# The last attention's schedule: projections in odd steps, prologue pieces in even ones, an earlier normalisation, the output bias as a weight row and the mask in parts

## The chip, the cores and the metric

The kernel runs on one core of a Trainium2 chip. Its time is the device time of the whole program on that core, in microseconds (us). The core has five engines that work beside each other: TensorE (PE, with its weight loads shown as PEld), VectorE (DVE), ScalarE (ACT), GpSimd (POOL) and SyncE (SP), which issues the transfers. Each engine takes its instructions in order, and an instruction waits for what others must have written or freed. Everything here is float32.

## The reference

The input is x, 8 batches of 512 rows with 256 columns. Four layers follow one another, each with its own normalisation and added to x: an attention (a), a feed-forward block with local attention, a second attention (b), and the feed-forward block again. Only attention b is changed. It has 16 heads of 16 columns, a score that is no plain product, and a bias on its output:

```python
    def _L0_attn_b_ref(x, w_qkv, b_qkv, w_out, b_out):
        ...
        qkv = x @ w_qkv + b_qkv
        q, k, v = jnp.split(qkv, 3, axis=-1)
        ...
        dot = jnp.einsum('bhid,bhjd->bhij', q, k)
        q_norm_sq = jnp.sum(q * q, axis=-1, keepdims=True)
        k_norm_sq = jnp.sum(k * k, axis=-1, keepdims=True)
        vals = q_norm_sq + k_norm_sq.transpose(0, 1, 3, 2)
        scores = dot * dot / (vals - 2.0 * dot + EPSILON) * SCORE_SCALE
        mask = jnp.triu(jnp.ones((Lq, Lq), dtype=scores.dtype), k=1) * -1000000000.0
        scores = scores + mask[None, None, :, :]
        attn = jax.nn.softmax(scores, axis=-1)
        out = jnp.einsum('bhij,bhjd->bhid', attn, v)
        out = out.transpose(0, 2, 1, 3).reshape(Bq, Lq, E)
        return out @ w_out + b_out
    ...
    x = x + _L0_attn_b_ref(_layernorm(x, axis=-1), L0_attn_b_w_qkv, L0_attn_b_b_qkv, L0_attn_b_w_out, L0_attn_b_b_out)
```

## The kernel before

The eight batches are done in two groups of four, whose rows stay in SBUF (`xs`). A group passes through ten stages: attention a, two layers of local attention and feed-forward, attention b (`attention_b`, L946), and two such layers again. Each stage gives a head and a function `run`; in its last steps `run` calls `ahead`, which writes the next stage's head in between.

**Units and steps.** In attention b a batch is cut into 22 units. A unit is a block of 128 query rows (`i`, 0 to 3) with a pair of heads from each of several groups of four heads (`js`): for `i` = 0 there are two units of four pairs, for `i` = 1 four units of two pairs, for `i` = 2 and 3 eight units of one pair each. With the causal mask a block `i` needs `i` + 1 blocks of keys, so each unit has 1024 scores in a row (768 for `i` = 2). `each_part` (L1253) writes one step, in which up to six units are in work at different depths: the denominators of unit s (`product`, then `inverse` on ScalarE, `error` and `refine` on VectorE), the square of the dot product of unit s-1 (`squares`, L1112, which also adds the mask `causal` on POOL at L1116), the maximum of unit s-2 (`highest`, L1119, VectorE) and its exponentials on ScalarE, the transposes of unit s-3 in two halves, each copied to SBUF by VectorE (`keep_turned`, L1157), and in odd steps the products with the values of units s-5 and s-4 (`values`).

**Pieces.** Each step may take one piece of other work, cut into up to four parts that are put in between: `first` on TensorE, `act` on ScalarE, `second` on TensorE, `dve` on VectorE. There are two kinds:

- *Projections* (`project`, L1184). When all heads of a block `i` are done, the reciprocal of the sums is spread on POOL, and two pieces follow: one turns the reciprocals and divides (`oT`, L1205), one multiplies by the output weights (`pp`, L1210) and adds to x (L1215). They come up in steps 5, 9, 17 of a batch and in step 3 of the next.
- *The prologue of the next batch* (`stacks_and_values`, L964): one piece that turns the normalised rows into columns, eight *side pieces* (`side_piece`, L981) that make the stacks for q and k, marked heavy, with TensorE, ScalarE, TensorE and VectorE in a chain (`pu_b` L987, `sq_b` L997, `pu_b` L1000, `st_b` L1013), and two *value pieces* (`value_piece`, L1024).

Ahead of the prologue come two pieces that only VectorE and POOL work on (`normalized`, L949): the statistics (four `bn_stats` and aggregates, then two POOL instructions for the inverse root), and the rows (`yr`), with the output bias then added to x on POOL (L959).

**Which piece a step takes** is decided by `a_piece` (L1246):

```python
if projections:
    return projections.popleft()
if prologues and not norms and not (with_values and prologues[0].heavy):
    return prologues.popleft()
```

So a projection always goes first, and a heavy piece never goes into a step with value products, which is every odd step from the fifth on. At the start of a batch (`step % each == 0`, L1308) what is left of its prologue is written out at once, piece after piece (`whole`, L1059); I call this the drain. Only then do `norms` and `prologues` get the pieces of the batch after it. `kept_order` makes the order in which the steps are written the order on every engine.

**Buffers.** Denominators, dot products and the pieces share three PSUM buffers (`ps_s`); the transposes have one (`ps_mm`).

Of the kernel before, what the change touches and what calls it, by code (L numbers as in the profile page):

```python
# [17 lines left out]
P = 128  # L18
NB, T, D = 8, 512, 256
NT = T // P  # L20
GROUP = 4
H, HD = 8, 64
HB, HDB = 16, 16
# [21 lines left out]
def kernel(  # L45
# [12 lines left out]
    b_wv,  # L58
    b_bv,
    b_wo,  # L60
    b_bo,
    f_wqkv,
    f_scale,
    f_wo,
# [38 lines left out]
    def part(flat, at, shape):  # L103

        n = int(np.prod(shape))
        view = flat[:, at : at + n]
        if len(shape) == 2:
            view = view.rearrange("p (k n) -> p k n", n=shape[1])
        return view, at + n

    def fetch(src, dst, rows=True):
        nc.sync.dma_start(dst, src.rearrange("(k p) n -> p k n", p=P) if rows else src.partition_broadcast(P))
# [55 lines left out]
    def weights_b(name):  # L168
        flat = wts.tile([P, 4096], F32, tag="wa", name=f"wb_{name}", bufs=2)
        wl, at = part(flat, 0, (2, INNER))  # L170
        wr, at = part(flat, at, (2, INNER))
        wv, at = part(flat, at, (2, D))
        wo, at = part(flat, at, (4, D))
        bv, at = part(flat, at, (D,))
        bo, at = part(flat, at, (D,))
        for s, d in ((b_wl, wl), (b_wr, wr), (b_wv, wv), (b_wo, wo)):
            fetch(s, d)
        fetch(b_bv, bv, False)
        fetch(b_bo, bo, False)
        return wl, wr, wv, wo, bv, bo  # L180


    ident = const.tile([P, P], F32, name="ident")
# [760 lines left out]


    def attention_b(batches, g):  # L946
        wl_b, wr_b, wv_b, wo_b, bv_b, bo_b = weights_b(g)

        def normalized(b):  # L949

            got = {}

            def statistics():
                got["mv"], got["rstd"] = row_statistics([xs[b]], f"b{b}")

            def rows():
                yr = pool.tile([P, NT, D], F32, tag="yr", name=f"yr_b{b}", bufs=1)
                normalize_rows([xs[b]], [yr], got["mv"], got["rstd"])
                nc.gpsimd.tensor_add(xs[b], xs[b], bo_b.unsqueeze(1).to_broadcast([P, NT, D]))  # L959
                state[b] = {"yr": yr}  # L960

            return [Piece(False, dve=statistics), Piece(False, dve=rows)]

        def stacks_and_values(b):  # L964


            got = {}

            def turned():
                got["pt"] = ps_s.tile([P, 2, NT, P], F32, tag="s", name=f"pyt_b{b}")  # L970
                for k in range(2):
                    for t in range(NT):
                        nc.tensor.transpose(got["pt"][:, k, t, :], state[b]["yr"][:, t, k * P : (k + 1) * P], ident)

            def columns():
                got["yT"] = pool.tile([P, 2, T], F32, tag="hT", name=f"yT_b{b}")
                nc.scalar.copy(got["yT"], got.pop("pt").rearrange("p k t c -> p k (t c)"))

            yield Piece(False, first=turned, act=columns)

            def side_piece(side, w, j):  # L981
                vec = vec_b[:, side, j, :]

                def project():
                    got["pu"] = ps_s.tile([P, 2, T], F32, tag="s", name=f"pu_b{b}_{side}_{j}")[:, 0]
                    for k in range(2):
                        nc.tensor.matmul(  # L987
                            got["pu"],
                            lhsT=w[:, k, j * P : (j + 1) * P],
                            rhs=got["yT"][:, k, :],  # L990
                            start=(k == 0),
                            stop=(k == 1),
                        )

                def squared():
                    got["sq"] = pool.tile([P, T], F32, tag="two", name=f"sq_b{b}_{side}_{j}", bufs=5)
                    nc.scalar.activation(got["sq"], got["pu"], AF.Square, bias=vec[:, 0:1])  # L997

                def norms():
                    nc.tensor.matmul(  # L1000
                        got["pu"],
                        lhsT=sel_b[:, side, :],
                        rhs=got.pop("sq"),
                        start=False,
                        stop=True,
                        skip_group_check=True,
                    )

                def keep_side():
                    name = ("left", "right")[side]  # L1010
                    if name not in state[b]:
                        state[b][name] = big([P, 4, T], f"st_b{b}_{side}")
                    nc.vector.tensor_scalar(  # L1013
                        state[b][name][:, j, :], got.pop("pu"), vec[:, 0:1], vec[:, 1:2], ALU.add, ALU.mult
                    )

                return Piece(True, project, squared, norms, keep_side)

            for side, w in ((0, wl_b), (1, wr_b)):
                for j in range(4):  # L1020
                    yield side_piece(side, w, j)


            def value_piece(t2):  # L1024
                def project():
                    got["pv"] = ps_s.tile([P, 2, 2, HB * HDB], F32, tag="s", name=f"pv_b{b}_{t2}")
                    for i in range(2):
                        t = 2 * t2 + i
                        for k in range(2):
                            nc.tensor.matmul(  # L1030
                                got["pv"][:, i, 0],
                                lhsT=got["yT"][:, k, t * P : (t + 1) * P],
                                rhs=wv_b[:, k, :],
                                start=(k == 0),
                                stop=(k == 1),
                            )

                def keep_values():
                    if t2 == 0:
                        state[b]["v"] = pool.tile([P, NT, (HB + 1) * HDB], F32, tag="v", name=f"v_b{b}")  # L1040
                        nc.gpsimd.memset(state[b]["v"][:, :, HB * HDB :], 0.0)
                    pv = got.pop("pv")
                    for i in range(2):
                        nc.vector.tensor_add(state[b]["v"][:, 2 * t2 + i, : HB * HDB], pv[:, i, 0], bv_b)

                return Piece(False, first=project, dve=keep_values)

            for t2 in range(NT // 2):
                yield value_piece(t2)
# [16 lines left out]
        def unit(b, i, qp, js, first, last):  # L1066
# [8 lines left out]
            def per_head(t):  # L1075
                return t[:, :, :cols].rearrange("p a (m w) -> p a m w", w=width)
# [35 lines left out]
            def squares(dot):  # L1112
                num = pool.tile([P, 2, T], F32, tag="p", name=f"num_{n}", bufs=3)
                nc.scalar.activation(num[:, :, :cols], dot[:, :, :cols], AF.Square, scale=-0.5)  # L1114
                own = per_head(num)[:, :, :, past:]
                nc.gpsimd.tensor_add(own, own, causal.unsqueeze(1).unsqueeze(1).to_broadcast([P, 2, len(js), P]))  # L1116
                return num

            def highest(num, r):  # L1119
# [109 lines left out]
        def run(ahead):  # L1229
# [13 lines left out]
                        if k < len(some):  # L1243
                            some[k]()

            def a_piece(with_values):  # L1246
                if projections:
                    return projections.popleft()
                if prologues and not norms and not (with_values and prologues[0].heavy):
                    return prologues.popleft()  # L1250
                return Piece(False)

            def each_part(s):  # L1253
# [6 lines left out]
                if with_values:  # L1260
                    for u in (s - 5, s - 4):
                        projections.extend(units[u].project(sums.pop(u)))
                piece = a_piece(with_values)

                def do(part):
                    if part:
# [40 lines left out]
            for step in range(count + 5):  # L1307
                if step % each == 0:  # L1308
                    with kept_order():
                        while prologues or norms:  # L1310
                            whole((norms or prologues).popleft())
                    following = step // each + 1
                    if following < len(batches):
                        norms.extend(normalized(batches[following]))
                        prologues = deque(stacks_and_values(batches[following]))
                with kept_order():
                    each_part(step)
                if step > count - 6:
                    ahead()
# [48 lines left out]
def laid_out(inputs):  # L1368
# [17 lines left out]
    vec = vec.reshape(2, 4, P, 2).transpose(2, 0, 1, 3)  # L1386
    wo_b = np.zeros((HB, 2, HDB, D), f)
    wo_b[:, 0] = i["L0_attn_b_w_out"].reshape(HB, HDB, D)

    qs, ks = i["L0_ffn_q_scale"], i["L0_ffn_k_scale"]  # L1390
    swapped = lambda s: np.concatenate([s[:, HD // 2 :], s[:, : HD // 2]], 1)
# [2 lines left out]
    for half, rest in ((0, 0), (1, GATES)):  # L1394
# [17 lines left out]
        "b_wv": wqkv[:, 2 * D :],  # L1412
        "b_bv": bias[2 * D :],
        "b_wo": wo_b.reshape(INNER, D),
        "b_bo": i["L0_attn_b_b_out"],
        "f_wqkv": i["L0_ffn_wqkv"],
        "f_scale": np.stack([qs, swapped(qs), ks, swapped(ks)], 1),
        "f_wo": i["L0_ffn_wo"],
# [25 lines left out]
```

## Time and profile before

| | |
|---|---|
| median of 3 runs | 4722.27 us (4718.59 to 4723.31) |
| profiled execution | 4716.77 us, span 4715.0 us |
| granted TensorE clock, mean | 0.963 |
| busy: PE, PEld | 4385.6 us (93%), 2660.9 us (56%) |
| busy: DVE, ACT, POOL | 3177.9 us (67%), 2243.9 us (48%), 1275.0 us (27%) |
| attention b, first group | from about 1081 to 1600 us |
| attention b, second group | from about 3425 to 3950 us |

The page divides the span into 40 slices of 118 us; each digit is the tenths of a slice in which the engine was busy. Attention b lies in slices 9 to 13 and 29 to 33, counted from 0. The rows of its instruction groups name the line, the engine, the tile written and the tiles read; their mean is in nanoseconds. The answers of the trace that are used below are of three kinds: busy times of each engine in chosen stretches, with the granted clock (PEclk, 1.00 is full speed); VectorE's waits, as "who waited <- for what: us in total, times, longest"; and instructions in order of time, with start, duration and, in brackets, the idle time in front and what ended it.

### The profile page before, as it was taken

How to read it: one execution, taken by the hardware profiler on the slowest of the kernel's cores; microseconds unless marked ns; L12 is line 12 of the kernel's file. 1: busy time of each engine (PE TensorE's matmuls, PEld its weight loads, DVE VectorE, ACT ScalarE, POOL GpSimd, SP SyncE). 2: the span in 40 equal slices, each digit the busy share in tenths (PEclk: the TensorE clock that was granted, in tenths of full speed). 3: DMA queues.
4: the chain of work that ended last, by engine and by line, in shares of the span. 5: the costliest groups of instructions: out<-in, count | busy, mean ns of one | idle time of the engine just before them, and what ended most of it. 6: DMA issues, size and time to landing. Idle time of an engine off the chain costs nothing. (4 is left out here: it accounts for less than half of the span.)

```text
span 4715.0 us, 68722 instructions
## 1 busy us (share of the span) xinstructions
PE 4385.6 (93%) x26240; PEld 2660.9 (56%) x26240; DVE 3177.9 (67%) x7400; ACT 2243.9 (48%) x5228; POOL 1275.0 (27%) x1164
## 2 busy tenths in 40 slices
PE   9999999997777899999999999999977778999999
PEld 5666656654444466566566666566544444665665
DVE  5667637738998777377456686476389887863772
ACT  3345425417877654155133453254178775541541
POOL 0014314312222243133100242243122222431431
PEclk9999999999988799999999999999989887999999
DMA  2000000000000000000100000000000000000000
GB/s 77 1 21 3 23 21 3 21 5 19 1 1 1 19 3 5 4 21 12 49 28 1 19 3 23 21 3 23 2 19 1 1 1 19 3 6 21 3 4 23
DMA packets 50922, 63.17 MB, mean 13 GB/s; under 512 B 6257, under 2 KB 45345, under 8 KB 50593
## 3 DMA queue, kind: packets, MB, share of 16 engines
q1 hardware_dynamic: 50592, 58.77, 3.8%
q8 instruction: 208, 3.41, 0.3%
q14 instruction: 122, 0.99, 0.1%
HBM read 46.19 MB, written 4.19 MB: 11 GB/s over the span
## 5 line engine op out<-in xcount | busy, mean ns | idle before, releaser
L1154 PE MATMUL ppt_b<-ident,num_b 128*128 128x128 f32 x1280 | 249.4, 318 | 200.4 <-DVE pt_b L1159 157.7
L1154 PEld LDWEIGHTS ppt_b<-ident,num_b 128*128 128x128 f32 x1280 | 155.4, 157 | 383.6 <-ACT num_b L228 133.0
L1116 POOL TENSOR_TENSOR num_b<-num_b,causal 128x256 f32<-128x256 f32 (+2 forms) x176 | 172.0, 977 | 695.3 <-ACT num_b L1114 525.1
L228 ACT ACTIVATE p_a<-s_a,nm_a 128x512 f32<-128x512 f32 x256 | 173.8, 683 | 304.1 <-DVE nm_a L384 304.1
L228 ACT ACTIVATE num_b<-num_b,most_b 128x512 f32<-128x512 f32 (+3 forms) x512 | 280.7, 553 | 50.4 <-DVE most_b L1134 47.4
L1124 DVE CUSTOM_DVE_ANT_0 num_b<-num_b,r_b 128x512 f32<-128x512 f32 (+3 forms) x512 | 263.9, 562 | 4.6 <-POOL num_b L1116 4.6
L1085 PE MATMUL den_b<-st_b,st_b 18*128 18x384 f32 (+3 forms) x1024 | 238.6, 523 | 7.3 <-DVE t_b L1104 5.1
L1159 DVE COPY pt_b<-ppt_b 128x512 f32<-128x512 f32 (+1 forms) x352 | 223.3, 634 | 29.6 <-PE ppt_b L1154 28.5
L228 ACT ACTIVATE r_b<-den_b 128x1024 f32<-128x1024 f32 (+1 forms) x176 | 166.5, 946 | 150.1 <-PE den_b L1085 96.9
L1085 PE MATMUL dot_b<-st_b,st_b 16*128 16x384 f32 (+3 forms) x1024 | 216.0, 525 | 1.9 <-ACT num_b L1114 1.4
L228 ACT ACTIVATE p_f1y<-p_f1y,nm_f1y,rn_f1y 128x256 f32<-128x256 f32 (+1 forms) x256 | 143.7, 563 | 137.5 <-DVE nm_f1y L617 125.7
L228 ACT ACTIVATE p_f0y<-p_f0y,nm_f0y,rn_f0y 128x256 f32<-128x256 f32 (+1 forms) x256 | 143.7, 564 | 137.3 <-DVE nm_f0y L617 125.7
L228 ACT ACTIVATE p_f0x<-p_f0x,nm_f0x,rn_f0x 128x256 f32<-128x256 f32 (+1 forms) x256 | 143.7, 564 | 130.1 <-DVE nm_f0x L617 118.4
L228 ACT ACTIVATE p_f1x<-p_f1x,nm_f1x,rn_f1x 128x256 f32<-128x256 f32 (+1 forms) x256 | 143.7, 564 | 129.9 <-DVE nm_f1x L617 118.4
L1104 DVE TENSOR_TENSOR t_b<-den_b,r_b 128x1024 f32<-128x1024 f32 (+1 forms) x176 | 196.7, 1118 | 10.8 <-ACT r_b L228 9.8
L1108 DVE SCALAR_TENSOR_TENSOR r_b<-t_b,r_b 128x1024 f32<-128x1024 f32 (+1 forms) x176 | 198.1, 1126 | 0.1
L384 DVE TENSOR_REDUCE nm_a<-s_a 128x2 f32<-128x1024 f32 x128 | 156.2, 1221 | 62.3 <-PE s_a L380 61.1
L228 ACT ACTIVATE r_b<-r_b 128x1024 f32<-128x1024 f32 (+1 forms) x176 | 172.4, 980 | 5.5
L397 PEld LDWEIGHTS ppt_a<-ident,p_a 128*128 128x128 f32 x1024 | 110.0, 141 | 98.0 <-ACT p_a L228 40.4
L1114 ACT ACTIVATE num_b<-dot_b 128x1024 f32<-128x1024 f32 (+1 forms) x176 | 164.7, 936 | 0.0
L399 DVE COPY pt_a<-ppt_a 128x1024 f32<-128x1024 f32 x128 | 155.5, 1215 | 2.6 <-PE ppt_a L397 2.5
L853 PE MATMUL pu_g0x<-hT_g0x,wg_0x 128*128 128x512 f32 (+1 forms) x352 | 157.3, 594 | 0.0
(349 smaller groups left out, 11025.8 us busy)
## 6 DMA issues: line engine op xcount, KB each, us to landing
x<-in_x SPq DMA_DIRECT2D x8, 512.0 KB
out<-x SPq DMA_DIRECT2D x8, 512.0 KB
wf_0x<-in_f_wqkv SPq DMA_DIRECT2D x2, 1536.0 KB
wf_0y<-in_f_wqkv SPq DMA_DIRECT2D x2, 1536.0 KB
wf_1x<-in_f_wqkv SPq DMA_DIRECT2D x2, 1536.0 KB
wf_1y<-in_f_wqkv SPq DMA_DIRECT2D x2, 1536.0 KB
wg_0x<-in_f_w SPq DMA_DIRECT2D x2, 1386.0 KB
wg_0y<-in_f_w SPq DMA_DIRECT2D x2, 1386.0 KB
```

Source lines behind the costliest of these rows:

```text
L228: i = nc.scalar.activation(out, in_, func, **more).ins
L384: nc.vector.tensor_reduce(nm, s, AX.X, ALU.max, negate=True)
L399: nc.vector.tensor_copy(pt, ppt)
L853: nc.tensor.matmul(pu[: cols.stop - cols.start, c], lhsT=w1[:, k, cols], rhs=hT[:, k, :], start=(k == 0), stop=(k == 1),)
L1085: return nc.tensor.matmul(s[:, a, m * width : (m + 1) * width], lhsT=left[at, j, past:width], rhs=right[at, j, :width], start=True, stop=True,
L1104: nc.vector.tensor_mul(t[:, :, :cols], den[:, :, :cols], r[:, :, :cols])
L1108: nc.vector.scalar_tensor_tensor(r[:, :, :cols], t[:, :, :cols], 2.0, r[:, :, :cols], ALU.subtract, ALU.mult)
L1114: nc.scalar.activation(num[:, :, :cols], dot[:, :, :cols], AF.Square, scale=-0.5)
L1116: nc.gpsimd.tensor_add(own, own, causal.unsqueeze(1).unsqueeze(1).to_broadcast([P, 2, len(js), P]))
L1124: nc.vector.tensor_tensor_reduce(out=s4[:, a, m, :], in0=s4[:, a, m, :], in1=r4[:, a, m, :], scale=-1.0, scalar=LOWEST, op0=ALU.mult, op1= ...
L1154: nc.tensor.transpose(ppt[:, k, :], p[:, a, k * P : (k + 1) * P], ident)
L1159: nc.vector.tensor_copy(pt[:, a, :nblocks, :], ppt[:, :nblocks, :])
```

## The change

Five edits, all for attention b:

1. `a_piece` takes a projection in an odd step, or in an even one when an even number of projections waits; else a prologue piece, if the next batch's normalised rows exist and the step isn't an odd one (after step 4 of the stage) with a heavy piece in front; else a projection that is left over.
2. The statistics and rows of a batch's normalisation are put two steps before the start of the batch in front of it (step 20 of 22); only those of the second batch still come at the first batch's start.
3. The bias is no longer added on POOL nor loaded. The column block behind the last head's values is filled with 1 instead of 0, so that the product with the exponentials gives their sum there, and after the division 1; the matching row of the output weights holds the bias.
4. The mask is added per pair of heads (`m`), in instructions of 128x256, in place of one for the whole unit.
5. The argument of `a_piece` is the step.

```diff
-        fetch(b_bo, bo, False)
-        return wl, wr, wv, wo, bv, bo
+        return wl, wr, wv, wo, bv
...
                 normalize_rows([xs[b]], [yr], got["mv"], got["rstd"])
-                nc.gpsimd.tensor_add(xs[b], xs[b], bo_b.unsqueeze(1).to_broadcast([P, NT, D]))
                 state[b] = {"yr": yr}
...
-                        nc.gpsimd.memset(state[b]["v"][:, :, HB * HDB :], 0.0)
+                        nc.gpsimd.memset(state[b]["v"][:, :, HB * HDB :], 1.0)
...
-                own = per_head(num)[:, :, :, past:]
-                nc.gpsimd.tensor_add(own, own, causal.unsqueeze(1).unsqueeze(1).to_broadcast([P, 2, len(js), P]))
+                for m in range(len(js)):
+                    own = per_head(num)[:, :, m, past:]
+                    nc.gpsimd.tensor_add(own, own, causal.unsqueeze(1).to_broadcast([P, 2, P]))
...
-            def a_piece(with_values):
-                if projections:
-                    return projections.popleft()
-                if prologues and not norms and not (with_values and prologues[0].heavy):
-                    return prologues.popleft()
+            def a_piece(s):
+                ready = prologues and batches[s // each + 1] in state and not (s % 2 and s > 4 and prologues[0].heavy)
+                for some, may in ((projections, s % 2 or len(projections) % 2 == 0), (prologues, ready), (projections, True)):
+                    if some and may:
+                        return some.popleft()
                 return Piece(False)
...
-                        norms.extend(normalized(batches[following]))
+                        if following == 1:
+                            norms.extend(normalized(batches[1]))
                         prologues = deque(stacks_and_values(batches[following]))
+                elif step % each == each - 2 and step // each + 2 < len(batches):
+                    norms.extend(normalized(batches[step // each + 2]))
...
     wo_b[:, 0] = i["L0_attn_b_w_out"].reshape(HB, HDB, D)
+    wo_b[HB - 1, 1, 0] = i["L0_attn_b_b_out"]
```

More of the change, by code (lines that the diff above doesn't have):

```diff
@@ L60 @@
     b_wo,
-    b_bo,
     f_wqkv,
@@ L174, in weights_b @@
         bv, at = part(flat, at, (D,))
-        bo, at = part(flat, at, (D,))
         for s, d in ((b_wl, wl), (b_wr, wr), (b_wv, wv), (b_wo, wo)):
@@ L946, in attention_b @@
     def attention_b(batches, g):
-        wl_b, wr_b, wv_b, wo_b, bv_b, bo_b = weights_b(g)
+        wl_b, wr_b, wv_b, wo_b, bv_b = weights_b(g)
         def normalized(b):
@@ L1262, in each_part @@
                         projections.extend(units[u].project(sums.pop(u)))
-                piece = a_piece(with_values)
+                piece = a_piece(s)
                 def do(part):
@@ L1414, in laid_out @@
         "b_wo": wo_b.reshape(INNER, D),
-        "b_bo": i["L0_attn_b_b_out"],
         "f_wqkv": i["L0_ffn_wqkv"],
```

## The prediction, made before the changed kernel ran

> **What bounds the kernel.** I read the page's slices first: TensorE is busy in nine tenths nearly everywhere, but in slices 9 to 13 and 29 to 33 (from 0) it falls to seven or eight tenths while VectorE rises to seven, eight and nine. That is the last attention, which runs once per group of four batches; the change touches nothing else. So I asked for busy times by stretch, cut at the first group's batch boundaries:
>
> ```profile
> core 0: us, PE busy (x) PEld busy (x) DVE busy (x) ACT busy (x) POOL busy (x), PEclk, DMA share, GB/s
> 1085.00:1202.00 117.00, 89.08 (x686) 48.07 (x686) 111.88 (x249) 96.29 (x194) 30.63 (x28) 0.91 0.02 5
> 1202.00:1212.00 10.00, 6.91 (x47) 5.15 (x46) 5.93 (x13) 3.87 (x5) 0.05 (x1) 1.00 0.01 2
> 1212.00:1328.00 116.00, 89.45 (x798) 53.43 (x797) 113.10 (x260) 99.15 (x200) 33.01 (x30) 0.93 0.00 1
> 1328.00:1346.00 18.00, 13.35 (x59) 7.23 (x58) 7.75 (x16) 5.27 (x9) 0.00 (x0) 1.00 0.00 0
> 1346.00:1467.00 121.00, 93.64 (x800) 56.32 (x800) 118.95 (x280) 99.12 (x201) 35.57 (x35) 0.86 0.00 1
> 1467.00:1486.00 19.00, 14.35 (x78) 8.02 (x80) 8.75 (x17) 6.27 (x11) 0.69 (x1) 1.00 0.00 0
> 1486.00:1600.00 114.00, 95.35 (x726) 57.89 (x724) 103.61 (x236) 90.78 (x189) 25.82 (x26) 0.73 0.00 1
> ```
>
> Inside a batch VectorE works 111.88 of 117, 113.10 of 116, 118.95 of 121 us: it is the bound, with ScalarE (99 of 116) and TensorE behind. Only in a group's last batch, at clock 0.73, does it have air. Between batches stand short stretches in which VectorE is more than half idle. VectorE's waits in 1327 to 1346, then in 1487 to 1600:
>
> ```profile
> DVE st_b L1013 <- PE pu_b L1000: 8.3, 3, 2.8
> DVE v_b L1044 <- PE pv_b L1030: 1.9, 2, 1.0
> ...
> DVE pt_b L1159 <- PE ppt_b L1154: 8.0, 9, 2.4
> ```
>
> The first two are the drain at a batch boundary: pieces of the next batch's prologue that found no step are run one after another by `whole`, each a chain of TensorE, ScalarE, TensorE, VectorE with nothing beside it. The instructions in order of time show three side pieces (3.62 us apart) and two value pieces in each of the second and third drains, one side and two value pieces in the first.
>
> **Part 1, the drain.** VectorE's waits there are 2.7 + 1.9 = 4.6 us in the first drain and 8.3 + 1.9 = 10.2 in each other, 25.0 us per group; the second group gives the same numbers. Twice is 50.0 us. Only this idle time can go: the 0.81 us per side piece and 0.76 per pair of value additions move with the pieces, into steps where VectorE is the bound.
>
> Does everything find a place? I followed the new rule by hand. In a first batch the eight side pieces run in steps 3, 4, 6, 8, 10, 12, 14, 16, the value pieces in 18 and 20. In later ones the columns are turned in the batch's first step, the sides go in its steps 2, 4, 8, 10, 12, 14, 16, 18 (counted from 0) and the values in 20 and 21. The built order of the changed kernel agrees: nothing stands between the batches, and TensorE has as many instructions as before. This needs the statistics two steps early (steps 20 and 21), else the columns could not be turned in a batch's first step. They are the same VectorE instructions (four statistics of 0.39 us, four aggregates of 0.17, four row operations of 0.41) plus two on POOL (1.07 and 1.35 us) behind which one mask waits for less than a step: cost 0. If POOL were late, the mask of a step that VectorE reads only in the next one would be, so up to 2 us per batch.
>
> What the filled steps cost: some 7 side and 6 value pieces per group are new in steps, and 11 second projection halves (`pp`, four products, 1.89 us together on TensorE) move into odd steps, which also hold the value products. For a full-width odd step I add from the rows around 1174 to 1187: products 1.1, two transposes 1.3, value products 0.9 to 1.1, `pp` 1.89, together 5.2 to 5.4 us; VectorE's own in such a step is 1.21 + 1.38 + 0.17 + 1.36 + 1.21 = 5.3 us plus 0.41 for the addition, 5.7. So TensorE still fits, with 0.3 to 0.5 us to spare. A side piece in a step costs VectorE today some 0.35 us of wait (1.1 us in three, in the waits of 1213 to 1327). With 0.35 for the sides, 0.3 for values, 0.2 for the moved halves: 2.5 + 1.8 + 2.2 = 6.5 us per group, 13 for both, as an estimate. Ends: 0 (all hidden) and 48 (first rival). Part 1: -50 + 13 = **-37 us**.
>
> **Part 2, the bias.** `tensor_add` on POOL (L959) goes; a constant 1 beside the last head and a row of the weights take its place, in columns that the products already cover, so nothing is added. POOL is not the bound, but it shuts VectorE out:
>
> ```profile
> 1221.42 1.22 DVE L1108 SCALAR_TENSOR_TENSOR r_b<-t_b,r_b 128x1024 f32<-128x1024 f32 x1
> 1222.56 0.29 DVE L1124 CUSTOM_DVE_ANT_0 num_b<-num_b,r_b 128x128 f32<-128x128 f32 x1
> 1222.77 2.44 DVE L1124 CUSTOM_DVE_ANT_0 num_b<-num_b,r_b 128x128 f32<-128x128 f32 x1
> ...
> 1225.56 2.42 DVE L1124 CUSTOM_DVE_ANT_0 num_b<-num_b,r_b 128x128 f32<-128x128 f32 x1
> ...
> 1221.59 3.46 POOL L959 TENSOR_TENSOR x<-x,wb 128x1024 f32<-128x1024 f32 x1 [1.30 <-PE ppt_b L1154]
> 1225.49 2.34 POOL L1116 TENSOR_TENSOR num_b<-num_b,causal 128x1024 f32<-128x1024 f32 x1 [0.44 <-ACT num_b L1114]
> ```
>
> The instruction of 0.28 us takes 2.44 while POOL adds the bias, and ends 0.15 us after POOL's. Six of the eight additions lie so (the other two before a stage begins): 6 x 2.16 = 13 us, in stretches where VectorE is busy 13.86 of 14.00 us (1346 to 1360). I take **-11**; ends -13 and 0 (if what VectorE then waits for is late).
>
> **Part 3, the mask in parts.** POOL's instructions by form:
>
> ```profile
> L1116 POOL TENSOR_TENSOR num_b<-num_b,causal 128x256 f32<-128x256 f32 x128 | 93.3, 729 | 561.4 <-ACT num_b L1114 426.4 <-issue 135.0
> L1116 POOL TENSOR_TENSOR num_b<-num_b,causal 128x512 f32<-128x512 f32 x32 | 40.8, 1275 | 117.8 <-ACT num_b L1114 82.6 <-issue 35.2
> L1116 POOL TENSOR_TENSOR num_b<-num_b,causal 128x1024 f32<-128x1024 f32 x16 | 37.9, 2368 | 16.1 <-ACT num_b L1114 16.1
> ```
>
> Sixteen of 2.37 us become 64 of 0.73, thirty-two of 1.28 become 64: 80 more instructions at 729 - (1275 - 729) = 183 ns fixed cost, 14.6 us more on POOL. Today the widest ones stretch VectorE's instructions (over their usual time, each under a mask of 1024) by 12.8 us in the maxima, 4.2 in the small scaling, 3.9 in the row operations, 2.5 in the refinement, 23.4 in all; the 512 ones stretch none, the 128 small ones 0.7 us together. Here a rule speaks against the edit. The Trainium skill, "GPSIMD Engine Reference", section "2.1 Instruction dispatch", says that each instruction pays its dispatch in software; section "8. Key points" that POOL shares its SBUF interfaces with VectorE, in contention with instructions that have two SBUF inputs. By the rule all 14.6 us more could fall on VectorE: +15. By the row, masks of 256 cost it almost nothing, because they fall beside its work from PSUM; and one of 0.73 us can hold a maximum up a third as long as one of 2.37, though several may be held up in turn. The row is nearer: **-6**, a quarter of 23.4; ends -23 and +70 (third rival).
>
> The clock is the other place. After the drain the granted clock is 0.50 (1346 to 1360). "TensorE: Matmul & The Clock Gate", section "HAM oscillation — how this bites in real kernels", says that TensorE's gaps over about 3.4 us halve its clock. By the rule, closing the gaps returns half of TensorE's 9.36 us, some 4.7, at each of six boundaries: -28. By the row VectorE is busy 13.86 of 14.00 us there, so a faster TensorE ends nothing earlier: 0, which I take.
>
> **Sum.** -37 - 11 - 6 = -54: from the profiled 4716.8 us to 4663. The median of the runs shown lies 5.5 us above the profiled execution, so about 4668.
>
> **Rivals.**
> - *TensorE takes over.* The filled steps hold 19 pieces in 22 steps instead of 14, and each holds a third score buffer, so the next denominators must wait until VectorE has freed theirs (L1085 already waits for `t_b` 43 times, 26.8 us in all). For: TensorE's spare is 0.3 to 0.5 us at full clock and gone at 0.9. Against: clock 1.00 from 1410 to 1466, where today's filled steps lie. Price: the last batch's 8.0 us of wait in each of six batches, 48 instead of 13: -50 + 48 - 11 - 6 = -19, 4703.
> - *More comes free.* No new waits, all POOL stretching gone, the last batch's 8.0 us too because no drain chills the clock: -50 - 13 - 23 - 16 = -102, 4620. Against: in the last batch the clock stays low 100 us after the drain.
> - *Slower: the masks shut VectorE out in turn.* If each part stops a maximum, the first two units of a batch lose 4 x 0.73 = 2.92 instead of 23.4/16 = 1.46, +23 for all 16 units; the next four lose 1.46 instead of nothing (+47 for 32). With parts 1 and 2: -37 - 11 + 70 = +22, 4744. It decides from 48/48 = 1.0 us per multi-head unit. Against: the 512 masks stretch nothing today.
> - *The bias never reaches the output or the drain stays.* The built order excludes the second; the first costs no time.
>
> **Chances.** Forecast 0.61, TensorE 0.17, more 0.15, slower 0.07. A measurement of this kernel can't tell less than about 0.2% (9.4 us) from no change. Faster 0.87, same 0.06 (TensorE's case gone further), slower 0.07. Range 4630 to 4706: up to TensorE's case, and most of the way to the best one.
>
> **What would show it.** Right: no stretch between batches with VectorE under 80% busy; no 2 us instruction under L959; masks of 256 without VectorE rows over 1 us. The stage, from 1085 to 1600 today, some 26 us shorter in each group. Wrong: `pt_b` or `st_b` waits that grow to over 20 us a group (TensorE), or maxima of 128 columns with a mean above today's 501 ns (masks).

## The result, and the profile after

The changed kernel takes 4660.97 us (median of 4 runs, 4657.26 to 4662.14) against 4721.77 us: 60.8 us less, a ratio of 0.9871 with a 95% interval of 0.9854 to 0.9888. The prediction had 4668, range 4630 to 4706. The profiled executions stand 55.3 us apart (4716.77 and 4661.49 us).

Practically all of these 55.3 us lie in the two passes of attention b. I measured each from its first denominator product to its last projection addition, and in it the time in which VectorE had an instruction in work (profiled executions, both groups together, us):

| kernel | passes | VectorE busy | VectorE idle | rest of the program |
|---|---|---|---|---|
| before | 1117.5 | 984.0 | 133.4 | 3597.5 |
| changed | 1062.3 | 963.8 | 98.6 | 3597.4 |
| difference | -55.2 | -20.2 | -34.8 | -0.1 |

Busy times by stretch of the changed kernel, first group: four stretches that end at the batch boundaries, then the first microseconds of the second, third and fourth batch. Columns as before: start and end, length, PE, PEld, DVE, ACT, POOL, granted clock, DMA share, GB/s.

```profile
1085.00:1205.00 120.00, 98.86 (x724) 54.86 (x724) 113.70 (x264) 96.07 (x194) 32.11 (x39) 0.89 0.01 3
1205.00:1332.00 127.00, 105.23 (x856) 61.48 (x854) 119.78 (x281) 103.81 (x207) 34.62 (x42) 0.90 0.00 1
1332.00:1462.00 130.00, 109.68 (x877) 65.28 (x872) 122.98 (x287) 107.47 (x213) 31.59 (x40) 0.89 0.00 1
1462.00:1575.00 113.00, 92.54 (x735) 55.50 (x737) 103.01 (x238) 90.99 (x190) 28.43 (x36) 0.78 0.00 1
...
1205.00:1220.00 15.00, 12.69 (x126) 8.94 (x122) 14.27 (x39) 11.78 (x17) 5.61 (x5) 0.76 0.00 1
...
1332.00:1350.00 18.00, 16.00 (x137) 12.07 (x132) 18.00 (x53) 12.00 (x18) 4.58 (x5) 0.63 0.01 2
...
1462.00:1480.00 18.00, 13.18 (x135) 9.79 (x137) 16.83 (x49) 13.14 (x31) 8.29 (x10) 0.59 0.01 3
```

The stretches between the batches are gone; the second and third batch are 11 and 9 us longer, since they hold the pieces, and VectorE is busy in 94 to 95% of the first three. The last three lines show a thing to keep: the clock at the start of a batch is low (0.76, 0.63, 0.59) although no drain stands in front of it any more; in the kernel before it was 0.76, 0.50 and 0.69 in the same first microseconds after its three drains. The changed kernel around the first boundary, and TensorE's instruction there (in brackets, the idle time in front of it):

```profile
1195.00:1202.00 7.00, 3.43 (x47) 1.88 (x45) 6.83 (x19) 4.43 (x8) 3.36 (x4) 1.00 0.00 0
1202.00:1208.80 6.80, 5.95 (x37) 5.05 (x38) 6.62 (x15) 3.86 (x7) 0.33 (x1) 0.50 0.00 0
...
1202.31 1.09 PE L1152 MATMUL ppt_b<-ident,num_b 128*128 128x128 f32 x4 [3.87 <-DVE pt_b L1157]
```

TensorE now stands still in front of a boundary because it waits for VectorE: 3.87 us here, 3.89 and 2.75 us at the next two. Towards the end of each of these waits the clock goes from 1.00 to 0.50.

The groups of VectorE's instructions say which idle time went. Kernel before (busy us, mean ns, then idle us in front of the group and who ended it):

```profile
L1159 DVE COPY pt_b<-ppt_b 128x512 f32<-128x512 f32 x224 | 153.0, 683 | 25.1 <-PE ppt_b L1154 24.0
...
L1013 DVE TENSOR_SCALAR st_b<-pu_b,vec_b 128x512 f32<-128x512 f32 x64 | 51.8, 810 | 86.2 <-PE pu_b L1000 86.2
...
L1044 DVE TENSOR_TENSOR v_b<-pv_b,wb 128x256 f32<-128x256 f32 x32 | 12.1, 419 | 13.8 <-PE pv_b L1030 13.8
```

The changed kernel, same groups:

```profile
L1157 DVE COPY pt_b<-ppt_b 128x512 f32<-128x512 f32 x224 | 153.0, 683 | 36.0 <-PE ppt_b L1152 34.6
...
L1009 DVE TENSOR_SCALAR st_b<-pu_b,vec_b 128x512 f32<-128x512 f32 x64 | 51.8, 809 | 52.0 <-PE pu_b L996 51.3
...
L1041 DVE TENSOR_TENSOR v_b<-pv_b,wb 128x256 f32<-128x256 f32 x32 | 11.9, 413 | 2.5 <-PE pv_b L1027 2.5
```

The side and value pieces make VectorE wait 34.2 + 11.3 = 45.5 us less; the transposes make it wait 10.9 us more in the form shown and 11.7 in all. The net, 33.8, is nearly all of the table's 34.8. The wait didn't vanish, a quarter of it changed its name.

The new waits for transposes are few and long. In the second and third batches of both groups they are 15.3 us, where they were 1.2; four of them, of 2.3 to 2.6 us each, make up 9.8. The first:

```profile
1246.40:1253.20 6.80, 6.80 (x24) 4.22 (x23) 5.78 (x15) 5.87 (x19) 1.89 (x3) 0.50 0.00 1
...
1249.66 3.62 PE L1208 MATMUL pp_b<-wb,oT_b 128*128 128x256 f32 x8
...
1254.92 0.69 DVE L1157 COPY pt_b<-ppt_b 128x512 f32<-128x512 f32 x1 [2.46 <-PE ppt_b L1152]
```

A projection's second half, now in an odd step, meets a stretch of half the clock: it takes 3.62 us, not the 1.89 that the prediction read at full clock, and the value products and transposes come behind it. The clock falls here too as a wait of TensorE ends (2.08 us, for VectorE).

### The profile page after: what moved, and what is told of

Read it like the earlier page. It is cut to its first block, busy times and chain, and to the rows that moved or that the text cites. A ratio compares the mean times of both kernels' runs of the same rounds, so it can differ in the third digit from the quotient of the medians.

```text
span 4659.7 us, 68806 instructions
## 1 busy us (share of the span) xinstructions
PE 4386.4 (94%) x26240; PEld 2659.4 (57%) x26240; DVE 3157.6 (68%) x7400; ACT 2240.2 (48%) x5228; POOL 1270.5 (27%) x1236
## 5 line engine op out<-in xcount | busy, mean ns | idle before, releaser
L1114 POOL TENSOR_TENSOR num_b<-num_b,causal 128x256 f32<-128x256 f32 x256 | 197.0, 782 | 664.8 <-ACT num_b L1111 573.7
L225 ACT ACTIVATE num_b<-num_b,most_b 128x512 f32<-128x512 f32 (+3 forms) x512 | 280.7, 554 | 24.0 <-DVE most_b L1132 20.1
L1122 DVE CUSTOM_DVE_ANT_0 num_b<-num_b,r_b 128x512 f32<-128x512 f32 (+3 forms) x512 | 249.5, 533 | 5.4 <-POOL num_b L1114 5.4
L381 DVE TENSOR_REDUCE nm_a<-s_a 128x2 f32<-128x1024 f32 x128 | 156.1, 1220 | 60.8 <-PE s_a L377 59.6
L850 PE MATMUL pu_g1x<-hT_g1x,wg_1x 128*128 128x512 f32 (+1 forms) x352 | 157.3, 594 | 0.0
```

The lines of the kernel that those rows point to most:

```text
L225: i = nc.scalar.activation(out, in_, func, **more).ins
L381: nc.vector.tensor_reduce(nm, s, AX.X, ALU.max, negate=True)
L850: nc.tensor.matmul(pu[: cols.stop - cols.start, c], lhsT=w1[:, k, cols], rhs=hT[:, k, :], start=(k == 0), stop=(k == 1),)
L1114: nc.gpsimd.tensor_add(own, own, causal.unsqueeze(1).to_broadcast([P, 2, P]))
L1122: nc.vector.tensor_tensor_reduce(out=s4[:, a, m, :], in0=s4[:, a, m, :], in1=r4[:, a, m, :], scale=-1.0, scalar=LOWEST, op0=ALU.mult, op1= ...
```

## The experiments

Twelve kernels ran, all but one of them with an edit; each ratio is to the kernel before on the same chip. What every kind of edit does to the time:

| kernel | us | ratio to before, 95% interval |
|---|---|---|
| drain alone | 4672.98 | 0.9900 (0.9885 to 0.9915) |
| bias alone | 4697.85 | 0.9952 (0.9940 to 0.9965) |
| mask alone | 4715.09 | 0.9990 (0.9983 to 0.9996) |
| changed | 4660.97 | 0.9871 (0.9854 to 0.9888) |
| changed, mask whole | 4660.54 | 0.9871 (0.9858 to 0.9885) |
| changed, late statistics | 4662.56 | 0.9877 (0.9863 to 0.9890) |
| changed, projections first | 4693.82 | 0.9945 (0.9932 to 0.9959) |
| changed, mask whole and placed | 4661.41 | 0.9880 (0.9866 to 0.9893) |
| changed, more work in the last batch | 4657.56 | 0.9873 (0.9860 to 0.9887) |
| changed, run again | 4659.81 | 0.9873 (0.9858 to 0.9888) |
| changed, mask whole, no copies | 4656.38 | 0.9867 (0.9850 to 0.9883) |
| the same with more work in the last batch | 4642.53 | 0.9839 (0.9824 to 0.9854) |
| changed, mask whole, more work in the last batch | 4663.27 | 0.9885 (0.9866 to 0.9904) |

**Each part alone.** The theory was that VectorE bounds attention b, so that its idle time and what POOL holds it up by are all that counts. The new `a_piece` and the earlier statistics in the kernel before:

> The kernel before with edits 1, 2 and 5 alone: the drain goes into the steps, bias and masks stay as they were. Theory (VectorE is the bound in attention b, so the time is its idle time plus what POOL holds up): VectorE's waits for pu_b and pv_b fall by 45 us and its waits for the transposes grow by 12, as in the changed kernel: -33 to -40 us, ratio 0.992. Rival (the edits work only together, since the bias addition shuts VectorE out in the steps that are now full): -20 us or less, ratio above 0.9955.

Measured: 47 us less. In its profiled execution VectorE idles 96.1 us in the passes, 37 less than before, as the theory had it, and is busy 976.6, 7 less, which it had not: the time lies outside its range. The rival, that the drain can't be filled while the bias is added on POOL, falls.

The bias as a weight row in the kernel before:

> The kernel before with edit 3 alone: no bias addition on POOL. Theory (POOL's additions hold VectorE up by 6 x 2.16 us): -11 to -13 us, ratio 0.9975. Rival (POOL's work is hidden, what VectorE loses there it wins back at its next wait): within 3 us of the kernel before.

Measured: 22 us less, nearly twice what the theory had, though of its sign. VectorE is busy 962.1 us in the passes, 21.9 less, and idles no less (135.3). The rest comes from the masks, as the order of time shows. Kernel with the bias alone, at the place that the prediction showed:

```profile
1220.31 0.28 DVE L1120 CUSTOM_DVE_ANT_0 num_b<-num_b,r_b 128x128 f32<-128x128 f32 x1
...
1221.79 0.28 DVE L1120 CUSTOM_DVE_ANT_0 num_b<-num_b,r_b 128x128 f32<-128x128 f32 x1
...
1224.91 2.58 DVE L1104 SCALAR_TENSOR_TENSOR r_b<-t_b,r_b 128x1024 f32<-128x1024 f32 x1
...
1224.06 2.35 POOL L1112 TENSOR_TENSOR num_b<-num_b,causal 128x1024 f32<-128x1024 f32 x1 [6.26 <-ACT num_b L1110]
```

All eight maxima of the unit take 0.28 us. Without the 2.2 us that the bias took, VectorE is ahead when the mask starts, and the mask meets VectorE's work from PSUM first and then the refinement (2.58 instead of 1.2 us). Over the kernel the mean of the 128 narrow maxima falls from 501 to 299 ns (25.9 us), while the refinements get 7.7 us longer. The rows of the maxima, before and with the bias alone:

```profile
L1124 DVE CUSTOM_DVE_ANT_0 num_b<-num_b,r_b 128x128 f32<-128x128 f32 x128 | 56.5, 501 | 0.0
...
L1120 DVE CUSTOM_DVE_ANT_0 num_b<-num_b,r_b 128x128 f32<-128x128 f32 x128 | 30.7, 299 | 0.0
```

This run also shows that VectorE bounds the passes: 21.9 us of its work less, with its idle time as before, make them 20.0 us shorter (1097.5).

The mask in parts in the kernel before, and the changed kernel with the mask whole again:

```diff
-                for m in range(len(js)):
-                    own = per_head(num)[:, :, m, past:]
-                    nc.gpsimd.tensor_add(own, own, causal.unsqueeze(1).to_broadcast([P, 2, P]))
+                own = per_head(num)[:, :, :, past:]
+                nc.gpsimd.tensor_add(own, own, causal.unsqueeze(1).unsqueeze(1).to_broadcast([P, 2, len(js), P]))
```

> The kernel before with edit 4 alone: the mask in parts of 128x256. Theory (parts hold VectorE up in turn, so only some 3 us of 23 go): -2 to -5 us, ratio 0.999, POOL 14 to 20 us busier. Rival one (the parts let VectorE through): -12 us or more, ratio below 0.9975. Rival two (they shut it out): slower by 10 us or more.

> The changed kernel with edit 4 undone: one mask instruction per unit. Theory: slower than the changed kernel by 2 to 5 us, 0.988 of the kernel before. Rival one: slower by 12 us or more. Rival two: faster by 10 us or more, since POOL's 80 additional instructions are gone.

Measured: 5 us less in the kernel before, where both rivals fall (the interval is 2 to 8 us). In its profiled execution the passes are not shorter, though (1118.8 us; VectorE busy 3.8 less, idle 5.3 more), so where the 5 us come from isn't shown. In the changed kernel no difference can be told (4660.5 against 4661.0 us); these runs can't tell some 10 us from nothing, so there the rivals only just fall, and the theory's 2 to 5 us stay open. What parts do is seen in the changed kernel's first unit of the second batch:

```profile
1215.80 1.23 DVE L1105 SCALAR_TENSOR_TENSOR r_b<-t_b,r_b 128x1024 f32<-128x1024 f32 x1
1216.96 0.82 DVE L1122 CUSTOM_DVE_ANT_0 num_b<-num_b,r_b 128x128 f32<-128x128 f32 x1
...
1217.71 0.80 DVE L1122 CUSTOM_DVE_ANT_0 num_b<-num_b,r_b 128x128 f32<-128x128 f32 x1
...
1218.44 0.28 DVE L1122 CUSTOM_DVE_ANT_0 num_b<-num_b,r_b 128x128 f32<-128x128 f32 x1
...
1214.54 3.82 POOL L1114 TENSOR_TENSOR num_b<-num_b,causal 128x256 f32<-128x256 f32 x4 [2.52 <-ACT num_b L1111]
```

and in the changed kernel with the mask whole, at the same step:

```profile
1211.19 2.19 DVE L1105 SCALAR_TENSOR_TENSOR r_b<-t_b,r_b 128x1024 f32<-128x1024 f32 x1
1213.31 0.28 DVE L1121 CUSTOM_DVE_ANT_0 num_b<-num_b,r_b 128x128 f32<-128x128 f32 x1
...
1209.93 2.37 POOL L1113 TENSOR_TENSOR num_b<-num_b,causal 128x1024 f32<-128x1024 f32 x1 [2.53 <-ACT num_b L1111]
```

A part and a VectorE instruction take turns: two maxima are held for 0.5 us each, and the four parts, 2.92 us when they run alone, take 3.82. The whole mask holds one refinement for 1.0 us. It is the same loss in another form. Summed over the passes (durations over the median of their form, with a mask beside them, attention b's own tiles) masks cost VectorE 23.7 us before (the prediction counted 23.4 and 0.7), 19.5 changed, 15.1 changed with the mask whole; the 4.4 us between the last two don't show in the time.

**The parts together.** They don't add up: alone they bring 47, 22 and 5 us, 74 in all, and the changed kernel brings 61. The changed kernel with the mask whole is drain and bias together, and it ran beside each of them on one chip: its 4660.54 us are 12.4 less than the drain alone and 37.3 less than the bias alone. VectorE's busy time in the passes shows the overlap: 7.4 us less with the drain alone, 21.9 with the bias alone, but only 23.2 with both (960.8). Each of the two edits also moves the masks away from the maxima, and that can be had once: counted as above, masks on the maxima cost 12.8 us before, 4.3 with the drain alone, and nothing with the bias alone or with both.

**Does the early normalisation matter?** The changed kernel with the statistics and rows where they were:

```diff
-                        if following == 1:
-                            norms.extend(normalized(batches[1]))
+                        norms.extend(normalized(batches[following]))
...
-                elif step % each == each - 2 and step // each + 2 < len(batches):
-                    norms.extend(normalized(batches[step // each + 2]))
```

> The changed kernel with edit 2 undone: statistics and rows in the first two steps of the batch in front, so the columns are turned in step 2 and each later piece moves back by one place. Theory (the early statistics cost nothing by themselves and are there to give places): in later batches one or two pieces are left for a drain, some 3 to 7 us of wait at each of four boundaries: slower than the changed kernel by 8 to 25 us. Rival (the early statistics also take VectorE's work out of the steps in which POOL's masks of 1024 hold it up): slower by more than 25 us. Rival (the order of the statistics makes no difference): within 4 us.

Measured: 1.6 us slower by the medians, well within the intervals. The rival that the order makes no difference fits best; the runs alone would not exclude the theory's 8 us, but the trace has nothing of its waits of 3 to 7 us. The pieces still fit but one: a value piece runs between two batches, and all that VectorE waits for from 1318 to 1345 us of this kernel is

```profile
DVE v_b L1041 <- PE pv_b L1027: 0.4, 1, 0.4
```

In both passes together the side and value pieces make VectorE wait 17.1 us here and 16.1 in the changed kernel.

**Do the projections have to leave the even steps?**

```diff
-                for some, may in ((projections, s % 2 or len(projections) % 2 == 0), (prologues, ready), (projections, True)):
+                for some, may in ((projections, True), (prologues, ready)):
```

> The changed kernel, but a waiting projection always goes before a prologue piece, as in the kernel before, so second halves take even steps again. Theory: each of four later batches and the two first ones loses two to four even steps, up to five pieces are left over at a boundary, and 4 to 10 us of wait come back at each of six boundaries: slower than the changed kernel by 20 to 40 us. Rival (TensorE is the bound in odd steps that hold both value products and a projection): the loss is less than 10 us, because the odd steps get shorter, and the waits of VectorE for the transposes fall by more than 10 us.

Measured: 33 us slower than the changed kernel, as the theory had it. The drain is back; VectorE's waits from 1195 to 1225 us of this kernel:

```profile
DVE v_b L1041 <- PE pv_b L1027: 1.9, 2, 1.0
DVE st_b L1009 <- PE pu_b L996: 1.4, 1, 1.4
```

That is one boundary of six; in the two passes together the side and value pieces make VectorE wait 48.4 us against 16.1, and it idles 120.9 us against 98.6. Its waits for transposes fall by 9 us, from 40 to 30, so odd steps do get lighter, but that is far from what the drain costs: TensorE had not taken over.

**Can the mask be put where it costs nothing?** For units with several heads a tiny POOL copy of VectorE's last write stands in front of a whole mask:

```diff
+            def masked(num, most):
+                if len(js) > 1 and most is not None:
+                    after = pool.tile([P, 1], F32, tag="after", name=f"after_{n}", bufs=2)
+                    nc.gpsimd.tensor_copy(after, most[:, 8:9])
+                own = per_head(num)[:, :, :, past:]
+                nc.gpsimd.tensor_add(own, own, causal.unsqueeze(1).unsqueeze(1).to_broadcast([P, 2, len(js), P]))
```

> The changed kernel with the mask whole again and placed: for the units with several heads a POOL copy of one column that VectorE's last maximum step writes stands in front of it, so the mask starts when VectorE turns to its work from PSUM (0.68 + 1.21 + 0.68 us, more than the 2.37 us of a mask). Theory (a mask costs VectorE time only where it meets instructions with two SBUF inputs): of the 20 us that masks hold VectorE up, most go: 10 to 18 us faster than the changed kernel. Rival (any POOL instruction beside VectorE costs it the same, wherever it lies; or the later mask delays the next maxima): no gain, or slower by up to 15 us.

Measured: nothing (4661.4 us). The copy is done at 1213.8, but the mask still starts at 1214.52, since it waits for ScalarE's square: it was never too early, it is too late by a microsecond, and the refinement takes 2.18 us, as without the copy (2.19). The experiment didn't do what it was made for, so it leaves open whether a mask that fits would gain.

**The clock of the last batch.** Steps of a group's last batch that have no piece get two products that nobody reads:

```diff
+            def warm():
+                pw = ps_s.tile([P, 2, T], F32, tag="s", name="pw_b")[:, 0]
+                for k in range(2):
+                    nc.tensor.matmul(pw, lhsT=wl_b[:, k, :P], rhs=wl_b[:, k, :], start=(k == 0), stop=(k == 1))
...
+                if count - each <= s < count:
+                    return Piece(False, first=warm)
```

> The changed kernel with additional products in those steps of a group's last batch that have no piece: two products of 128x512 into a score buffer that nobody reads (work is added, none left out). Theory (VectorE waits 7.7 us per group there for transposes because TensorE's granted clock is 0.81 in these steps, and it is low because TensorE has too little to do): the clock rises to over 0.95 and the waits shrink: 5 to 12 us faster. Rival one (the low clock has another cause): clock unchanged, slower by 10 to 40 us as TensorE gets 1.9 us more in some 15 steps per group. Rival two (the clock rises, but the work costs as much as it gives): within 5 us.

Measured: 4657.6 us, not told apart from the changed kernel, as rival two had it. The clock did rise. Changed kernel, last batch:

```profile
1480.00:1575.00 95.00, 79.35 (x604) 45.70 (x608) 86.18 (x190) 77.85 (x160) 20.14 (x26) 0.81 0.00 1
```

With the additional products:

```profile
1478.00:1570.00 92.00, 84.31 (x616) 46.60 (x614) 86.30 (x191) 76.60 (x156) 20.17 (x27) 0.97 0.00 1
```

From 0.81 to 0.97. From there to the end of each pass VectorE's waits for the transposes fall from 22.5 to 16.3 us, both groups together. But the next stage's first tiles (`ro_f0y`, `ro_f1y`), which VectorE works on in between, now make it wait 20.1 us for TensorE and POOL instead of 14.3: what the last batch won is given back to the head of the next stage. VectorE idles 100.0 us in the passes, no less than in the changed kernel.

**POOL's copies of the sums.** The spread of the reciprocals on POOL holds a maximum up 30 times, 12.3 us in all. A product of each head's column with the identity needs no copy:

```diff
-                rb = pool.tile([P, HB, 2 * HDB], F32, tag="two", name=f"rb_{n}", bufs=5)
-                nc.gpsimd.tensor_copy(rb, sums.unsqueeze(2).to_broadcast([P, HB, 2 * HDB]))
...
-                        nc.tensor.transpose(got["prt"][:, k, :], rows[:, k * P : (k + 1) * P], ident)
+                        for q in range(4):
+                            h = 4 * k + q
+                            nc.tensor.matmul(
+                                got["prt"][q * 32 : (q + 1) * 32, k, :],
+                                lhsT=sums[:, h : h + 1].to_broadcast([P, 2 * HDB]),
+                                rhs=ident,
+                                start=True,
+                                stop=True,
+                            )
```

It ran with the mask whole again, beside the changed kernel itself, and with the additional products of the last batch; a further run kept the copies:

> The changed kernel once more, beside the next two: 0.987 of the kernel before by every theory.

> The changed kernel with edit 4 undone and without the POOL copies that spread the reciprocal sums: TensorE multiplies each head's column, read 32 times, with the identity, 16 small products in place of 4 transposes of the spread tile. Theory (VectorE is the bound, and a POOL instruction that meets one with two SBUF inputs holds it up: 32 copies, 12 us): 9 to 15 us faster than the changed kernel, 0.984 of the kernel before, and no maximum of 256 to 512 columns above 0.75 us. Rival (TensorE is the bound in the odd steps, which get 12 more instructions each): same or slower than the changed kernel, with more waits of VectorE for transposes and quotients.

> As the kernel just described, with the additional products of the run on the last batch's clock (work is added, none left out). Theory: another 2 to 6 us faster, as the last batch's clock rises from 0.8 to over 0.95 and VectorE waits less for the transposes there. Rival (that gain was noise): within 2 us of the kernel without them.

> The changed kernel with edit 4 undone and the additional products in the last batch (work is added, none left out), but with POOL's copies of the sums kept: it tells which part of the gain of the best version needs the missing copies. Theory (without the copies VectorE asks for its transposes earlier, which pays only when TensorE's clock is high in the last batch; each alone brings 2 to 4 us, both together 17): about 4655 us, 0.9865 of the kernel before. Rival (the whole mask and the higher clock bring it, the copies nothing): about 4643 us, 0.984.

Measured: without the copies 3.4 us less than the changed kernel beside it, within the intervals and short of the theory's 9 to 15. VectorE is busy 953.2 us in the passes, 11.0 less than in that run of the changed kernel, as priced, but idles 5.0 more: in the first group's last batch it waits 11.2 us for transposes instead of 7.7. With the additional products these waits fall to 4.2 us, and the time falls by 14 us, more than the 2 to 6 expected: the kernel is at **4642.53 us** (4639.03 to 4648.89), 17 us under the changed kernel that ran beside it (4655.22 to 4662.64); the intervals of the two ratios lie just apart (0.9854 and 0.9858). With the copies and the products, on another chip, it is no faster than the changed kernel: 4663 us, above what theory and rival had. So the gain shows only with both edits. My reading is that the first takes work off VectorE and the second lets TensorE deliver in time; in the profiled executions VectorE is busy 15.9 us less than in that run of the changed kernel and idles 3.3 less. Of the 15.9, 4.9 come with the products; why they do, and how the 17 us divide between batches, I didn't settle.

## Why the prediction was right

*What bounds.* Right, but idle and busy time of any engine add up to the passes, so that -34.8 and -20.2 make -55.2 shows nothing by itself. What shows it is the bias alone: 21.9 us of VectorE's work less, 20.0 us of the passes less. One reading was loose: in the first stretch between batches VectorE was busy 5.93 of 10.00 us, not more than half idle.

*Part 1, -37 us.* Measured -34.8 us of idle time in the changed kernel, -37 with the drain alone. All 50 us of drain went. The new waits came to 16 us where I had 13: 4.5 at the side and value pieces (11.6 in steps before, 16.1 now) and 11.7 at the transposes. In time the drain alone gave 47 us and not 37, since VectorE was also busy 7 us less; on top of the bias it gave 37. That the odd steps could take the projections was right: with projections in even steps the kernel loses 33 us.

One step of it failed: "This needs the statistics two steps early". It doesn't; with late statistics one value piece is left over at a boundary, at 0.4 us of wait. I had followed the new rule with the early statistics only.

*Part 2, -11 us.* The sign and the 13 us of hold-up were right, and on top of the drain the bias gave 12.4. Alone it gave twice the term, 22 us (0.9952, 0.9940 to 0.9965): I counted what POOL's addition did to the instruction under it, and not that the delay put the next mask onto the maxima. With the drain filled most of that second gain is already there.

*Part 3, -6 us.* Mis-sized: within the changed kernel no gain can be told (0.9871 with and without). Taken alone it gave 5. The 4.2 us fewer under masks that I see in the changed kernel, and more, are there with the mask whole. The additional POOL work was 25 us and not 14.6 (masks busy 172.0 us before, 197.0 changed, since the parts are held up too), and it cost no time that can be measured: the rule on dispatch, with its +15, did not decide either.

*The sum.* That -54 came so near is partly luck. Taken in this order, the drain gave 10 us more than its term, the bias about its term, and the mask none of its 6. The prediction added its terms as if they did not meet, and drain and bias do.

*The clock, 0 us.* Closing the drains did return no clock at the batch starts, but my account of it was wrong in two places. The drains held no gap of TensorE longer than 2.31 us, and their clock was 1.00; in the changed kernel the clock is as low at batch starts, behind TensorE's waits of 2.75 to 3.89 us for VectorE. That such waits lower it fits these traces, and filling the idle steps of the last batch did raise it there, but at the batch starts no run tests it. And the clock isn't free for VectorE everywhere: the four waits of 2.3 to 2.6 us lie where a moved `pp` ran at half clock. At full clock each `pp` would take some 1.7 us less, so about 7 us in all hang on the clock, as an estimate from 3.62 and 1.89 us.

*Rivals.* "TensorE takes over": its sign was there in the longer waits for transposes, at 12 us of 48. Counted to the end of a pass they are 21.5 and 18.2 us per group, so in the first group the sign I had named, over 20 us, was just touched (13.9 and 14.6 before). "More comes free": no. "The masks shut VectorE out in turn": they do so, two or three in a row, at 0.5 us each, which is 12 us in all and not 70, and the maxima's mean is 390 ns, not above 501.

## What to carry to other kernels

Where one engine bounds a stage, add up its idle time by releaser and its instructions that take longer than their form does; their sum is what a new order can give, and what the filled steps make it wait for must be taken off. An instruction on a neighbouring engine that holds the bound one can cost more than its own overlap, since it also moves the next collision: take it away alone and measure before splitting the others. Gains of that kind don't add up, so measure the edits in pairs too: 47 and 22 us alone were 59 together. Where pieces have to be fitted into steps, count the places for the simple version too: here the early statistics could have stayed where they were.

## What the hardware showed that I had not expected

- POOL and VectorE take turns in both directions: four POOL additions of 128x256 that take 2.92 us alone took 3.82 between maxima, which took 0.8 instead of 0.28 us.
- A POOL copy with one input holds VectorE's maxima too (0.41 us each, 30 times).
- TensorE's granted clock was 0.59 to 0.76 in the first 15 to 18 us of a batch with TensorE busy in 73 to 89% of them and no drain ahead, behind waits of TensorE of 2.75 to 3.89 us. It rose from 0.81 to 0.97 in the last batch when each step without a piece got two more products.
- A projection's products that took 1.89 us at full clock took 3.62 at 0.50, and VectorE, otherwise busy in 94% of the batch, waited 2.46 us behind them.
